# Layernorm sums as three full products, a reordered convolution input, ordered spreads and new keys in a two-layer metaformer on one core

## The chip, the cores and the metric

The kernel runs on one core of one Trainium2 chip, in one launch. The metric is the device time in microseconds, the median of several runs. A core has five engines that run beside each other, each in the order of its own instruction list: TensorE (PE: matrix products, with weight loads shown apart as PEld), VectorE (DVE), ScalarE (ACT), GpSimd (POOL) and SyncE (SP), which here issues every DMA.

## The reference, cut to what matters

The input x is (8, 384, 32, 32) in float32. Everything is float32.

```python
# layer 0
x = x + L0_conv(ln_c(x), ...)           # a selective state space ("mamba") over the 1024 positions
t = to_tokens(x)
t = t + L0_ffn(ln_t(t), W1, b1, W2, b2)  # binarized weights, activations scaled by groups
x = from_tokens(t, x)
# layer 1
x = x + L1_conv(ln_c(x), offset)         # a shift per channel group, then a 5x5 Gauss filter
t = to_tokens(x)
t = t + L1_ffn(ln_t(t), W1, b1, W2, b2)
x = from_tokens(t, x)

def ln_c(v, eps=1e-6):                   # over the 384 channels; ln_t is the same with 1e-5
    m = mean(v, axis=1); s = var(v, axis=1)
    return (v - m) / sqrt(s + eps)

# the recurrence of L0_conv, for 768 inner channels d and 16 states n
dA = exp(dt_t[..., None] * A)
h = dA * h + (dt_t * u_t)[..., None] * B_t[:, None, :]
y = einsum('bdn,bn->bd', h, C_t)
```

The feed-forward part (FFN) works in five groups of the batch; the group size is 8 // 5 = 1, so its scaled output is zero for the last three images, and these need only the two convolutions.

## The kernel before, in words

Nothing is issued where it is written. A class Flow records each operation with its engine, the time that the author books for it, the buffers that it reads and writes, and a key; `Flow.run` then lays all operations out by a list schedule, engine by engine, and issues them in that order. In `run` the waiting operation with the smallest key goes next on its engine, provided its buffers can be had. Among equal keys the loop goes on to the end, so the one recorded last is taken. An operation that needs another table of ScalarE is charged a penalty (PEN) and may be held back for a while (HOLD). On the chip each engine then follows its list and waits on semaphores.

Keys are counted in scans. The state space is cut into 16 units (8 images, two halves of T = 512 positions). A unit has 6 channel blocks (JC) of 128, each with 4 groups of states (NG), so 24 scans a unit and 384 in all. A scan (`scan`) does two pairs p: POOL multiplies `t = dus * bc` (L868), ACT computes four decays (L878), DVE runs four recurrences (L893), POOL (L914) or DVE (L927) multiplies by C, and PE adds up four narrow products into y (L935). There are five t buffers, and a scan takes two.

dt and dt*u of a channel block lie as 128 channels and are needed as 32 channels repeated over four state groups. `spread` (L787) does that through DRAM: one DMA out to `via`, then eight back, four for each of the two pairs p, all with one key; it is called for dts and for dus, for two blocks at a time (`prep`).

Around the scans, all the rest is fitted in by keys: input projections (L645), for the last six units done early (`early`, L723) and kept in DRAM, the output projection (`end`, L997), and for each image the FFNs (first products L1386, second L1465) and the shifted convolution (`conv`). ROWS and CONVS give the key ranges of these per image; UNITS shifts four events of each unit and is all zeros.

`layernorm` (L491) sums over 384 channels on PE. A tile has 128 partitions and three chunks of channels, so `total` (L458) multiplies each chunk by a 128x32 block of ones, into three groups of 32 partitions of one PSUM bank (L464); ACT copies the 96 partitions to SBUF (L477); a second product with `pick`, which has ones in rows 0, 32 and 64, adds the three and spreads the result over all 128 partitions (L484). `layernorm` calls `total` twice, for the mean, which DVE then subtracts (L498), and for the squares that ACT makes (L512); ACT then takes Ln and Exp (L521, L529) and DVE multiplies (L537). There are 52 layernorms.

`conv` turns each 32x32 image by DVE's transposes of 32x32 blocks (L1569), multiplies by a matrix for the shift and filter along one axis (`ups`, L1601: two products of 256 columns), turns it back (L1615), multiplies for the other axis (`overs`, L1629: four of 128 columns), turns it once more (L1642), and POOL adds it to the residual (L1652). The tile `xt` that `ups` reads lies as (y, c) with c = 32, and `ups` reads it as (c, y): neighbours in its order are 32 elements apart. `overs` reads 16 neighbours at a time.

Of the kernel before, what the change touches and what calls it, by code (L numbers as in the profile page):

```python
# [17 lines left out]
P = 128  # L18
# [18 lines left out]

KB, KE, KC_, KY, KG = -0.73, 4.53, 0.68, -3.95, -25.21  # L40

KP, KR = -4.7, 10.49
KEND, KZ, KL, KX, KXP = 1.3, 23.33, -31.97, -2.16, -4.45

KI, KJ = 196.21, 703.54
EZ, EZ0, EZ1 = 6, -56.93, 53.6

AP, AD, AA, AL = 41.75, -45.76, -50.69, -258.62

PEN = 8.61  # L50

GBS = 260.0


ROWS = [
    [15.34, -7.72, -143.06, 131.51, -3.17, 59.74, -84.96, -78.05],
    [94.3, 121.48, 131.64, -65.6, 211.87, 125.27, 265.88, 164.43],
    [164.72, 212.1, 341.92, 181.75, 145.72, 247.03, 303.52, 178.27],
    [227.6, 313.23, 335.93, 52.96, 178.3, 308.14, 239.43, 298.28],
    [299.47, 295.45, 361.88, 314.75, 306.17, 351.8, 603.44, 450.53],  # L60
]
CONVS = [
    [202.4, 111.11],
    [759.94, 953.69],
    [430.57, 41.38],
]


UNITS = [
    [0.0, 0.0, 0.0, 0.0],  # L70
    [0.0, 0.0, 0.0, 0.0],
    [0.0, 0.0, 0.0, 0.0],
    [0.0, 0.0, 0.0, 0.0],
    [0.0, 0.0, 0.0, 0.0],
    [0.0, 0.0, 0.0, 0.0],
    [0.0, 0.0, 0.0, 0.0],
    [0.0, 0.0, 0.0, 0.0],
    [0.0, 0.0, 0.0, 0.0],
    [0.0, 0.0, 0.0, 0.0],
    [0.0, 0.0, 0.0, 0.0],  # L80
    [0.0, 0.0, 0.0, 0.0],
    [0.0, 0.0, 0.0, 0.0],
    [0.0, 0.0, 0.0, 0.0],
    [0.0, 0.0, 0.0, 0.0],
    [0.0, 0.0, 0.0, 0.0],
]


# [65 lines left out]
class Flow:  # L154
# [1 line left out]


    SWITCH = 1.5
    HOLD = {"exp": 0.0, "silu": 8.77, "gelu": 2.31, "softplus": 0.0}

    def __init__(self, nc):
        self.nc, self.ops, self.key, self.filler = nc, [], 0.0, None
# [200 lines left out]
def metaformer_flow(ctx, tc, x, mw, f0, offset, f1, out):  # L363
# [24 lines left out]
    op("POOL", 2.0, lambda e: make_identity(nc, ident.ap), (), [ident])  # L388


    pick = one("pick", [P, P])

    def first_rows(e):
        e.memset(pick.ap, 0.0)
        for q in range(Q):
            e.memset(pick.ap[q * D : q * D + 1, :], 1.0)

    op("POOL", 1.0, first_rows, (), [pick])


    mm = ring("mm", [P, T], 3, ps, ordered=False)
    y_r = ring("y", [P, T], 1, ps)
# [55 lines left out]
    def total(src, acc, sq):  # L458

        def chunks(eng):
            for k in range(KC):
                eng.matmul(  # L464
                    acc.ap[k * D : (k + 1) * D, :],
                    ones.ap[:, :D],
                    src.ap[:, k, :],
                    start=True,
                    stop=True,
                    tile_position=(0, k * D),  # L470
                )

        op("PE", 1.0, chunks, [ones, src], [acc], hold=[sq])
        op(
            "ACT",
            0.6,
            lambda eng: eng.copy(sq.ap[: KC * D, 0, :], acc.ap[: KC * D, :]),  # L477
            [acc],
            [sq],
        )  # L480
        op(
            "PE",
            1.0,
            lambda eng: eng.matmul(  # L484
                acc.ap, pick.ap[: KC * D, :], sq.ap[: KC * D, 0, :], start=True, stop=True
            ),
            [pick, sq],
            [acc],
        )

    def layernorm(tn, e):  # L491

# [69 lines left out]
    def load_x(i):  # L562
# [4 lines left out]
            return  # L567
        dma(lambda: t.ap, lambda: halves(x[b], s), (), [t], 768)

    fl.key = -60  # L570
    load_x(0)
    dma(lambda: cw.ap, lambda: conv_w.rearrange("(j p) t -> p j t", p=P), (), [cw], 10)

    def small(dst, src):
# [211 lines left out]

    def spread(src, r):  # L787

        via = via_r.new()
        dma(lambda: via.ap, lambda: src.ap, [src], [via])  # L790
        dst = [r.new(Q), r.new(Q)]
        for p in range(2):
            for q in range(Q):
                dma(
                    lambda p=p, q=q: dst[p].ap[q * D : (q + 1) * D],
                    lambda p=p: via.ap.rearrange("(c d) t -> d c t", d=D)[:, 2 * p : 2 * p + 2, :],
                    [via],
                    [dst[p][q]],
                    128,
                )  # L800
        return dst

    def prep(i, a):
# [204 lines left out]
    def state_space():  # L1008
        def at(i, j, g=0.0):
            fl.key = i * UNIT + j * NG + g  # L1010

        fl.key = -50
        ln(0)
        n0 = len(fl.ops)
        for j in range(JC):
            xin(0, j)
        weights.extend([o for o in fl.ops[n0:] if o.eng == "SP"][-1:])
        x_proj(0)
        n0 = len(fl.ops)
        load_bc(0, 0)  # L1020
        fl.key = -48
        prep(0, 0)
        started.extend(o for o in fl.ops[n0:] if o.eng == "SP" and o.key == -48)
        fl.key = -46
        n0 = len(fl.ops)
        for g in range(1, NG):
            load_bc(0, g)
        fl.key = -5
        zin(0, 0)
        zin(0, 1)  # L1030
        loads.extend(o for o in fl.ops[n0:] if o.wait == 0 or o.key == -46)
        for i in range(len(units)):
            nxt = i + 1 if i + 1 < len(units) else None
            for j in range(JC):
                for g in range(NG):
                    scan(i, j, g)
                    at(i, j, g)
                    if g == NG - 1 and j % 2 and i * JC + j + 1 < len(units) * JC:
                        fl.key += KP + UNITS[i][0]
                        prep(*divmod(i * JC + j + 1, JC))  # L1040
                        at(i, j, g)
                    if j == 0 and i > 0 and g == 0:
                        fl.key += KEND + UNITS[i][3]
                        end(i - 1)
                        at(i, j, g)
                    if j == 0 and g in (0, 2):
                        fl.key += KZ
                        zin(i, 2 + g)
                        zin(i, 3 + g)
                        fl.key -= KZ  # L1050
                    if nxt:
                        if j == 1 and g == 0:
                            fl.key += KL + UNITS[i][1]
                            load_x(nxt)
                            if nxt < LATE:
                                ln(nxt)
                            at(i, j, g)
                        if j in (2, 3, 4) and g in (0, 1):
                            fl.key += KX + UNITS[i][2]
                            xin(nxt, 2 * (j - 2) + g)  # L1060
                            at(i, j, g)
                        if j == 4 and g == 2:
                            fl.key += KXP + UNITS[i][2]
                            x_proj(nxt)
                            at(i, j, g)
                        if j == JC - 1:
                            load_bc(nxt, g)
                        if j == JC - 1 and g == 1:
                            fl.key += KZ
                            zin(nxt, 0)  # L1070
                            zin(nxt, 1)
                            fl.key -= KZ
                fl.key = i * UNIT + j * NG + NG + KG
                gate(i, j)
        end(len(units) - 1)


    def binarize(w, dst, kc, o):
# [6 lines left out]
        for g in range(NQ):  # L1085
# [40 lines left out]
                lambda e, z=z, s=s: e.activation(s.ap[:, :flat], z.ap[:, :flat], AF.Sign),  # L1126
                [z],
                [s],
            )
            op(  # L1130
                "POOL",
# [414 lines left out]
    def conv(src, dst, dst_ap):  # L1546

        xt = [hb_r.new(2) for _ in range(KC)]
        for s in range(NS):
# [14 lines left out]
            for c in range(KC):  # L1564
# [2 lines left out]
                    "DVE",  # L1567
                    0.7,
                    lambda e, c=c, tn=tn, ys=ys: e.transpose(  # L1569
                        xt[c].ap.rearrange("p (y c) -> p y c", c=32)[:, ys, :],  # L1570
                        tn.ap[:, c, :].rearrange("p (y x) -> p y x", x=32),
                    ),
                    [tn],
                    [xt[c][s]],
# [1 line left out]
        for c in range(KC):  # L1576
# [18 lines left out]
            for h in range(2):  # L1595
                acc = mm.new()

                def ups(e, lt=lts[0], acc=acc, h=h, c=c):
                    for k in (0, 1):
                        cs = slice(h * 16 + k * 8, h * 16 + k * 8 + 8)  # L1600
                        e.matmul(  # L1601
                            acc.ap.rearrange("p (c y) -> p c y", y=32)[:, k * 8 : k * 8 + 8, :],
                            lt.ap[:, 2 * h + k, :],
                            xt[c].ap.rearrange("p (y c) -> p c y", c=32)[:, cs, :],
                            start=True,
                            stop=True,
                        )

                op("PE", 1.0, ups, [lts[0], xt[c]], [acc], hold=[tr])
                hs = slice(h * T, (h + 1) * T)  # L1610

                op(
                    "DVE",
                    0.7,
                    lambda e, tr=tr, acc=acc, hs=hs: e.transpose(  # L1615
                        tr.ap[:, hs].rearrange("p (c x) -> p c x", x=32),
                        acc.ap.rearrange("p (c y) -> p c y", y=32),
                    ),
                    [acc],
                    [tr[h]],  # L1620
# [1 line left out]
            for h in range(2):  # L1622
# [3 lines left out]
                def overs(e, lt=lts[1], acc=acc, xs=xs, tr=tr):  # L1626
# [7 lines left out]
                            stop=True,  # L1634
                        )

                op("PE", 1.3, overs, [lts[1], tr], [acc])

                op(
                    "DVE",  # L1640
                    0.85,
                    lambda e, c=c, acc=acc, xs=xs: e.transpose(  # L1642
                        xt[c].ap.rearrange("p (x y) -> p x y", y=32)[:, xs, :],
                        acc.ap.rearrange("p (c x) -> p x c", x=16),
# [3 lines left out]
                )  # L1648
            op(
                "POOL",  # L1650
                2.35,
                lambda e, xr=xr, c=c: e.tensor_add(  # L1652
                    xr.ap.rearrange("p (y x) -> p y x", x=32),
                    xr.ap.rearrange("p (y x) -> p y x", x=32),
# [106 lines left out]
```

## Time and profile before

The three runs gave 3698.68, 3707.25 and 3713.39 us, the median being 3707.25.

| | us |
|---|---|
| profiled execution, its own time | 3705.44 |
| its span, first to last instruction | 3703.7 |
| mean granted TensorE clock, as a share of full speed | 0.923 |
| HBM read and written | 578.45 MB and 196.48 MB, 209 GB/s |

One execution was profiled. In its groups of instructions a line is the line of the kernel, or that of a helper that records: all DMAs of `dma` have L217, and most table loads L359. "out<-in" names what is written and read. A group's row ends with the idle time of its engine just before its instructions, and what ended it. PE's records overlap, so a group's busy time, in which overlaps count once, is less than its count times its mean. By stretches of the span, busy us of each engine:

| stretch, us | PE | DVE | ACT | POOL | clock |
|---|---|---|---|---|---|
| 0 to 78.6 (before the first scan) | 40.30 | 18.72 | 38.46 | 20.29 | 0.83 |
| 78.6 to 300 | 164.10 | 177.80 | 155.64 | 179.16 | 0.81 |
| 300 to 1000 | 594.77 | 588.38 | 508.20 | 621.70 | 0.91 |
| 1000 to 2000 | 900.20 | 844.96 | 702.93 | 874.83 | 0.95 |
| 2000 to 3000 | 862.04 | 874.36 | 671.94 | 877.58 | 0.93 |
| 3000 to 3634 | 572.93 | 547.48 | 405.90 | 562.72 | 0.94 |
| 3634 to 3703.7 (after the last scan) | 54.76 | 34.94 | 11.64 | 20.70 | 0.93 |

### The profile page before, as it was taken

Reading aid. Unit: us, or ns where it says so; the run is one execution under the profiler, and the core shown is the slowest. Engines: PE = TensorE matmul, PEld = TensorE weight load, DVE = VectorE, ACT = ScalarE, POOL = GpSimd, SP = SyncE. Lnnn points to the kernel's source line nnn. Section 1 sums busy time; section 2 is a strip of 40 time slices with the busy share of each in tenths; the row PEclk is TensorE's granted clock in tenths of the full one; section 3 lists DMA queues with packets and bytes.
Section 4 is the critical chain, followed back from the end, with each engine's and each line's share of the span. In section 5 each row is a group of like instructions: output and inputs, shape, how many; then the busy total and the mean of one; then the engine's idle time right before and its main releaser. Section 6 shows DMA issues by size and latency. Waiting matters only on the chain.

```text
span 3703.7 us, 35888 instructions
## 1 busy us (share of the span) xinstructions
PE 3189.1 (86%) x9572; PEld 1143.7 (31%) x9572; DVE 3086.6 (83%) x3080; ACT 2494.7 (67%) x3661; POOL 3157.0 (85%) x1680
## 2 busy tenths in 40 slices
PE   4777878987999897899979789998877999878988
PEld 1222223322333231333323233332223333323334
DVE  2798888878778889997987899889898888788986
ACT  4767886757667676677768757767665676765562
POOL 3879999897697998888899887989998788997893
PEclk7888979998999897999989899999988999988999
DMA  5858778696686886668587776969776787976964
GB/s 145 184 154 223 198 199 221 184 256 181 207 245 175 231 224 181 200 199 243 177 248 205 196 221 193 244 198 255 228 216 195 209 246 225 257 217 207 270 185 155
DMA packets 680820, 777.44 MB, mean 210 GB/s; under 512 B 113689, under 2 KB 434089, under 8 KB 680617
## 3 DMA queue, kind: packets, MB, share of 16 engines
q1 hardware_dynamic: 680616, 775.14, 74.4%
q8 instruction: 77, 1.26, 0.1%
q14 instruction: 127, 1.03, 0.1%
HBM read 578.45 MB, written 196.48 MB: 209 GB/s over the span
## 4 chain that ended last, share of the span: by engine, by line
PE 39%; DVE 16%; DMA 15%; POOL 12%; ACT 10%; issue 6%; SPq 2%; POOLq 0%; DVEq 0%; ACTq 0%
PE mm L1386 10%; PE mm L1465 9%; POOL t L868 8%; PE mm L645 6%; DVE dp L893 5%; PE y L935 4%; DMA dus<-via 3%; PE mm L997 3%; DVE t L893 3%; POOL t L914 3%; DVE t L927 3%; DMA dts<-via 2%; ACT L359 2%; ACT dp L878 2%; PE mm L1601 2%
## 5 line engine op out<-in xcount | busy, mean ns | idle before, releaser
L868 POOL TENSOR_TENSOR t<-dus,bc 128x1024 f32<-128x1024 f32 x768 | 1797.8, 2361 | 209.9 <-PE y L935 169.6
L914 POOL TENSOR_TENSOR t<-t,bc 128x1024 f32<-128x1024 f32 x384 | 906.8, 2362 | 99.6 <-DVE t L893 89.6
L935 PE MATMUL y<-t,sel 128*32 128x512 f32 x3072 | 554.9, 652 | 184.4 <-DVE t L927 117.8
L1465 PE MATMUL mm<-hb,w 128*128 128x512 f32 x1440 | 675.4, 609 | 28.4 <-DMA w<-w2d 12.1
L1386 PE MATMUL mm<-tn,w 128*128 128x512 f32 x1440 | 670.9, 611 | 24.7 <-DMA w<-w1d 7.5
L878 ACT ACTIVATE da<-dts,aneg 128x512 f32<-128x512 f32 x768 | 520.6, 684 | 240.7 <-DVE t L893 216.0
L878 ACT ACTIVATE dp<-dts,aneg 128x512 f32<-128x512 f32 x768 | 528.3, 688 | 207.2 <-DVE t L927 190.3
L893 DVE TENSOR_TENSOR_SCAN dp<-dp,h,t 128x512 f32<-128x512 f32 x384 | 491.3, 1279 | 71.7 <-ACT dp L878 53.5
L893 DVE TENSOR_TENSOR_SCAN dp<-dp,t 128x512 f32<-128x512 f32 x384 | 468.4, 1220 | 90.6 <-ACT dp L878 59.8
L893 DVE TENSOR_TENSOR_SCAN t<-da,h,t 128x512 f32<-128x512 f32 x384 | 481.2, 1267 | 64.2 <-POOL t L868 59.6
L893 DVE TENSOR_TENSOR_SCAN t<-da,t 128x512 f32<-128x512 f32 x384 | 458.2, 1206 | 79.5 <-POOL t L868 68.5
L359 ACT ACT_TABLE_LOAD x391 | 501.7, 1283 | 6.5
L645 PE MATMUL mm<-xn,win 128*128 128x512 f32 x900 | 439.3, 631 | 39.6 <-DMA win<-in_L_conv_in_proj_w 20.5
L927 DVE TENSOR_TENSOR t<-dp,bc 128x1024 f32<-128x1024 f32 x384 | 465.4, 1212 | 8.8 <-ACT h L920 4.0
L1465 PEld LDWEIGHTS mm<-hb,w 128*128 128x128 f32 x1440 | 264.9, 192 | 431.8 <-issue 352.7
L1386 PEld LDWEIGHTS mm<-tn,w 128*128 128x128 f32 x1440 | 269.4, 193 | 413.8 <-issue 311.5
L997 PE MATMUL mm<-z,wo 128*128 128x512 f32 x552 | 276.6, 634 | 12.2 <-DMA wo<-in_L_conv_out_proj_w 7.6
L645 PEld LDWEIGHTS mm<-xn,win 128*128 128x128 f32 x900 | 173.6, 200 | 294.7 <-issue 209.7
L1398 ACT ACTIVATE he<-mm,b 128x512 f32<-128x512 f32 x240 | 162.9, 680 | 148.9 <-PE mm L1386 141.6
L935 PEld LDWEIGHTS y<-t,sel 128*32 128x32 f32 x3072 | 83.4, 112 | 560.0 <-DVE t L927 201.1
L920 ACT COPY h<-dp 128x2 f32<-128x2 f32 x192 | 30.5, 159 | 218.4 <-DVE t L927 112.6
L1408 DVE TENSOR_REDUCE sm<-he 128x1 f32<-128x1024 f32 x120 | 144.3, 1203 | 30.8 <-ACT he L1398 30.2
(133 smaller groups left out, 3170.5 us busy)
## 6 DMA issues: line engine op xcount, KB each, us to landing
dts<-via SPq DMA_DIRECT2D x768, 128.0 KB, 4.4
dus<-via SPq DMA_DIRECT2D x768, 128.0 KB, 4.5
hd<-he SPq DMA_DIRECT2D x120, 512.0 KB, 4.7
hb<-hd SPq DMA_DIRECT2D x120, 512.0 KB, 5.9
via<-soft SPq DMA_DIRECT2D x192, 256.0 KB, 4.3
w<-w2d SPq DMA_DIRECT2D x120, 384.0 KB, 4.7
w<-w1d SPq DMA_DIRECT2D x240, 192.0 KB, 3.9
bc<-bcd SPq DMA_DIRECT2D x256, 128.0 KB, 4.7
```

Of the source, the lines that this page charges most:

```text
L359: nc.scalar.preload_act_table_set(SETS[table])
L645: e.matmul(acc.ap, w.ap[:, k, :], xn.ap[:, k, :], start=(k == 0), stop=(k == KC - 1))
L868: lambda e, t=t, du=du: e.tensor_mul(t.ap, du.ap, wide(0)),
L878: lambda e, c=c, r=r, dt=dt: e.activation(decay(c), dt.ap[:, r, :], AF.Exp, scale=aneg.ap[:, j * Q + c, g : g + 1],),
L893: e.tensor_tensor_scan(t.ap[:, r, :] if p == 0 else decay(c), decay(c), t.ap[:, r, :], 0.0 if s == 0 else hst[j][p].ap[:, g, r : r + 1], A ...
L914: op("POOL", 2.35, lambda e, t=t: e.tensor_mul(t.ap, t.ap, wide(1)), [bc], [t])
L927: lambda e, t=t: e.tensor_mul(t.ap, da[2].ap, wide(1)),
L935: e.matmul(y.ap[c * D : (c + 1) * D, :], sel.ap, ts[c // 2].ap[:, c % 2, :], start=(g == 0), stop=(g == NG - 1), tile_position=(0, c * D),)
L997: e.matmul(o.ap, flat()[:, j, :], zs[j].ap, start=(j == 0), stop=(j == JC - 1))
L1386: e.matmul(acc.ap, w.ap[:, k, :], tn.ap[:, k, :], start=(k == 0), stop=(k == KC - 1),)
L1398: lambda e, he=he, r=r, m=m, acc=acc: e.activation(he.ap[:, r, :], acc.ap, AF.Identity, bias=b1.ap[:, m : m + 1]),
L1465: e.matmul(acc.ap, w.ap[:, part * 2 + r, :], hs[m // 2].ap[:, r * T : (r + 1) * T], start=(m == 0), stop=(m == MC - 1),)
```

## The change

- `total` becomes three products of 128x128 ones with the three chunks, added up in one PSUM bank. The copy on ACT, the product with `pick` and `pick` itself go. The operation is booked at 1.83 us, where the two before were booked at 1.0 each.
- In `conv` the first transposes write `xt` as (k, y, c) with k = 4 and c = 8, so that `ups` reads 256 neighbours; the next transposes take `ups`' output in the new order. Some booked times around them change.
- In `spread` the eight DMAs get keys that rise with p, and those of dus come after those of dts of the same p. The first x load gets a key of its own, in front of the small weights.
- Sign in `binarize` is recorded as a user of the "exp" table.
- All the constants that shift keys, ROWS, CONVS, UNITS, PEN and HOLD get new values.

```diff
-KB, KE, KC_, KY, KG = -0.73, 4.53, 0.68, -3.95, -25.21
...
-PEN = 8.61
+KB, KE, KC_, KY, KG = -1.16, 5.28, 0.54, -7.6, -27.33
...
+PEN = 12.5
...
 UNITS = [
-    [0.0, 0.0, 0.0, 0.0],
...
+    [-1.66, -2.67, 2.76, -14.73],
+    [-2.83, 6.5, 1.53, 11.27],
...
-    HOLD = {"exp": 0.0, "silu": 8.77, "gelu": 2.31, "softplus": 0.0}
+    HOLD = {"exp": 0.0, "silu": 8.77, "gelu": 3.56, "softplus": 0.82}
...
-    pick = one("pick", [P, P])
...
     def total(src, acc, sq):
         def chunks(eng):
             for k in range(KC):
-                eng.matmul(
-                    acc.ap[k * D : (k + 1) * D, :],
-                    ones.ap[:, :D],
-                    src.ap[:, k, :],
-                    start=True,
-                    stop=True,
-                    tile_position=(0, k * D),
-                )
-
-        op("PE", 1.0, chunks, [ones, src], [acc], hold=[sq])
-        op(
-            "ACT",
-            0.6,
-            lambda eng: eng.copy(sq.ap[: KC * D, 0, :], acc.ap[: KC * D, :]),
-            [acc],
-            [sq],
-        )
-        op(
-            "PE",
-            1.0,
-            lambda eng: eng.matmul(
-                acc.ap, pick.ap[: KC * D, :], sq.ap[: KC * D, 0, :], start=True, stop=True
-            ),
-            [pick, sq],
-            [acc],
-        )
+                eng.matmul(acc.ap, ones.ap, src.ap[:, k, :], start=(k == 0), stop=(k == KC - 1))
+
+        op("PE", 1.83, chunks, [ones, src], [acc], hold=[sq])
...
+    fl.key = -62
+    load_x(0)
     fl.key = -60
-    load_x(0)
...
     def spread(src, r):
-        via = via_r.new()
+        via, k0 = via_r.new(), fl.key
         dma(lambda: via.ap, lambda: src.ap, [src], [via])
         dst = [r.new(Q), r.new(Q)]
         for p in range(2):
+            fl.key = k0 + 0.02 * p + (0.01 if r is dus_r else 0.0)
             for q in range(Q):
...
+        fl.key = k0
         return dst
...
                 lambda e, z=z, s=s: e.activation(s.ap[:, :flat], z.ap[:, :flat], AF.Sign),
                 [z],
                 [s],
+                table="exp",
...
-                        xt[c].ap.rearrange("p (y c) -> p y c", c=32)[:, ys, :],
-                        tn.ap[:, c, :].rearrange("p (y x) -> p y x", x=32),
+                        xt[c].ap.rearrange("p (k y c) -> p y k c", k=4, c=8)[:, ys],
+                        tn.ap[:, c, :].rearrange("p (y a b) -> p y a b", a=4, b=8),
...
                     for k in (0, 1):
-                        cs = slice(h * 16 + k * 8, h * 16 + k * 8 + 8)
                         e.matmul(
-                            acc.ap.rearrange("p (c y) -> p c y", y=32)[:, k * 8 : k * 8 + 8, :],
+                            acc.ap[:, k * 256 : k * 256 + 256],
                             lt.ap[:, 2 * h + k, :],
-                            xt[c].ap.rearrange("p (y c) -> p c y", c=32)[:, cs, :],
+                            xt[c].ap[:, (2 * h + k) * 256 : (2 * h + k + 1) * 256],
...
-                op("PE", 1.0, ups, [lts[0], xt[c]], [acc], hold=[tr])
+                op("PE", 0.75, ups, [lts[0], xt[c]], [acc], hold=[tr])
...
-                        tr.ap[:, hs].rearrange("p (c x) -> p c x", x=32),
-                        acc.ap.rearrange("p (c y) -> p c y", y=32),
+                        tr.ap[:, hs].rearrange("p (k c x) -> p k c x", k=2, x=32),
+                        acc.ap.rearrange("p (k y c) -> p k c y", k=2, c=8),
```

## The prediction

> **What bounds the kernel now.** First the page: busy shares, then the slices.
>
> ```profile
> PE 3189.1 (86%) x9572; PEld 1143.7 (31%) x9572; DVE 3086.6 (83%) x3080; ACT 2494.7 (67%) x3661; POOL 3157.0 (85%) x1680
> ...
> PE   4777878987999897899979789998877999878988
> ...
> POOL 3879999897697998888899887989998788997893
> PEclk7888979998999897999989899999988999988999
> ...
> PE 39%; DVE 16%; DMA 15%; POOL 12%; ACT 10%; issue 6%; SPq 2%; POOLq 0%; DVEq 0%; ACTq 0%
> ```
>
> Three engines are busy 83 to 86% and none fills the span of 3703.7 us: POOL, whose work the change leaves alone, is idle 547 us. So the time is POOL's 3157 us plus what POOL, PE and DVE lose by waiting for one another. The last line, the chain that ended last, runs over PE most (39%). The slices show where nothing can overlap: POOL's first slice is 3 and its last is 3. TensorE's clock is granted at 0.7 to 0.9 where PE has holes and at 9 where it is dense[...].
>
> Then the list of waits: who waited for whom, us in all, times, longest.
>
> ```profile
> POOL t L868 <- PE y L935: 169.6, 86, 8.4
> ...
> ACT sq L477 <- PE mm L464: 61.6, 36, 9.6
> ...
> PE mm L484 <- ACT sq L477: 37.9, 41, 2.0
> ```
>
> POOL's largest loss, 169.6 us, is for the y products: PE works in order, and what stands in front of a y product keeps t buffers from POOL. The other two lines are the layernorm sum's bounce, PE to ACT to PE. Then the groups, kept apart by shape (busy us, mean ns | idle before):
>
> ```profile
> L1386 PE MATMUL mm<-tn,w 128*128 128x512 f32 x1440 | 670.9, 611 | 24.7 <-DMA w<-w1d 7.5 <-DVE tn L537 6.4 <-ACT he L1398 4.4
> ...
> L359 ACT ACT_TABLE_LOAD x391 | 501.7, 1283 | 6.5
> ...
> L645 PE MATMUL mm<-xn,win 128*128 128x512 f32 x900 | 439.3, 631 | 39.6 <-DMA win<-in_L_conv_in_proj_w 20.5 <-DVE xn L537 4.5 <-DVE tr L1535 3.8
> ...
> L484 PE MATMUL mm<-sq,pick 96*128 96x512 f32 x208 | 128.3, 702 | 39.5 <-ACT sq L477 37.9 <-ACT h L920 1.5
> ...
> L1601 PE MATMUL mm<-hb,lt 128*128 128x256 f32 x192 | 89.2, 615 | 13.0 <-DVE hb L1569 8.4 <-DVE hb L1642 4.1 <-DVE xn L498 0.5
> ...
> L464 PE MATMUL mm<-sq,ones 128*32 128x512 f32 x312 | 64.2, 691 | 34.9 <-ACT sq L512 30.7 <-ACT tail L663 2.8 <-ACT soft L824 0.8
> ...
> L477 ACT COPY sq<-mm 96x512 f32<-96x512 f32 x104 | 60.1, 577 | 64.9 <-PE mm L464 61.6 <-PE y L935 1.5 <-ACT soft L824 0.6
> ...
> L464 PE MATMUL mm<-tn,ones 128*32 128x512 f32 x246 | 53.5, 731 | 31.8 <-DMA tn<-in_x 14.0 <-DMA tn<-x 9.7 <-ACT z L746 4.2
> L1629 PE MATMUL mm<-hb,lt 128*128 128x128 f32 x384 | 52.9, 289 | 7.3 <-DVE hb L1615 3.2 <-ACT dp L878 1.3 <-DVE hb L1642 0.9
> ```
>
> Every product leaves two records, so counts are halved below, and the mean of a record is no price: busy us over products is.
>
> **Part 1, the sums (104 of them, two in each of 52 layernorms).** Removed: three narrow products and one with pick. Their busy time is 64.2 + 53.5 + 14.5 (the third L464 row, on xn) + 128.3 = 260.5 us, 2.50 us a sum. Added: three full products, for which the trace has the same form. L1386: 670.9 us over 240 triples = 2.80 us. L645, with its second row of 16.6 us: 455.9 over 156 = 2.92 us. L723, more often cold: 120.1 over 36 = 3.34 us. I take L645, whose triples stand alone among scans as the sums do: 104 x (2.92 - 2.50) = **+44 us of PE**; the ends are +31 and +87. Here a rule speaks against the change: the Trainium skill (TensorE: Matmul & The Clock Gate, Part 3, row/col tiling) says narrow column tiles run concurrently and gives three of 32 columns at N=512 a speedup of 2.38. In this trace a warm narrow triple lasts 1.06 us; 2.38 x 1.06 = 2.52 us for the full one, and less the 1.06 and 1.02 of what goes that is +46 us. The timeline's warm full triples last 2.74 us, +69 us. All agree that PE gets more work.
>
> What it buys: ACT loses 104 copies, 60.1 us; PE's in-order wait for the copy (37.9 us idle) goes, and so does ACT's own 61.6 us idle for L464. From first narrow record to last pick record the timeline shows 2.9 us at best, 4.7 us in the cold start and over 10 us where pick stands behind other work (983.64 to 995.5); after, one piece of 2.7 to 5.3 us. What is late next is layernorm's DVE pass (L498) and Square, unchanged. On the path I count PE's +44 less the hole of 38, at PE's 39% of the chain: +2 us, and for the sooner sums -10 us (ends -40, 0): **-8 us**.
>
> **Part 2, convolution's first product (48 groups of two).** Before, its moving operand is read one element in 32. L1601 has 256 columns a record and takes 615 ns, as much as the 611 of 512 columns in L1386; L1629, which reads runs of 16, takes 289 for 128. So the stride, I conclude, halves the rate. A group now costs 89.2/48 = 1.86 us; in runs, by L1629's 52.9/384 = 0.14 us per record of 128, 4 x 2 x 0.14 = 1.1 us, by half of L1386's stream about 0.9. I take 0.95: 48 x 0.91 = **-44 us of PE**, ends 0 (the stride is not the cause) and -46. It weighs more than its size, since these groups come in convolution's bursts, where PE, DVE and POOL hand one tile round:
>
> ```profile
> 3683.51 3.47 PE mm L1601 x8
> 3687.77 1.16 PE mm L1629 x8
> 3688.93 3.71 PE mm L1601 x8
> 3694.36 2.78 POOL hb L1652
> ```
>
> These are pieces of the chain at its end; in the chain from 3560 us on L1601 alone holds 11.3%. Ten groups stand after the last y product. On the path I take half of the 44: **-22 us**. The transposes around it change pattern, not count. L1642 already reads PSUM with a step of 16 in 692 ns, L1615 without one in 706; I cost them at nothing (ends -2 and +10 us).
>
> **Part 3, the start.** Of equal keys the later recorded goes first, so the first x is now eighth on SP's queue:
>
> ```profile
> 5.20 0.55 SPq L217 DMA_DIRECT2D xn<-in_x  x1
> ...
> 10.87 1.93 PE L464 MATMUL mm<-xn,ones 128*32 128x512 f32 x6 [10.87 <-DMA xn<-in_x]
> ```
>
> With a key of its own it is issued first, at 0.74 us: -4.5 us on a stretch in which all wait for it. The small loads it passes (cw, cb, aneg) are wanted from 20 us on. Two cold sums cost about 2 x 0.6 us more. **-3 us.**
>
> **Part 4, ordered spreads.** By the same rule the second halves (p = 1) of dts and dus were issued before the first, which the scan needs first. Four issues of a median 0.42 us stand between: up to 1.7 us a tensor. The direct waits are small: DMA dus 8.6 us on POOL, dts 16.5 on ACT. I take -6 us, ends 0 and -25, the sum of those waits. No DMA is added.
>
> **Part 5, keys and table loads.** The program's order has 411 table loads for 396: 15 x 1.283 = +19 us of ACT. The skill (ScalarE: Activation LUTs, What ACT_TABLE_LOAD costs) adds a drain, 2.66 us a switch, which would be +40; but L359 shows 6.5 us idle before all 391, so 19 it is, inside ACT's 33% of idle: +3 us on the path at a load's share. In the order, PE has less behind the last y product: two sums instead of four, and 40 over products instead of 48. That is about 4 x 2.08 - 2 x 2.74 + 8 x 0.14 x 2 = 5 us, most in the tail: -4 us. The rest of the keys moves work between units of scans; instruction totals are equal, so I take 0, with ends of -60 and +60: about a third of the 169.6 us that POOL waits for y, either way.
>
> **Sum:** -8 - 22 - 3 - 6 + 3 - 4 = -40 from the profiled run's own 3705.4 us (its span of 3703.7 plus 1.7 around it), hence about 3665; part of any gain is usually lost to the next wait, so I forecast **3670 us**. The profiled run is 1.8 us under the median of 3707.25.
>
> **Rivals.**
> A, hidden: PE's +44 and -44 cancel, and ACT's relief is worth nothing at 67%. For it: the totals of POOL and DVE stay. Against: L1601 is on the chain, the start is too. Time: only the start and the tail, 3698.
> B, slower: full sums block the y products. The recording layer books a sum at 1.83 us but the same form at 2.65, so each is about 0.9 us longer than the order allows for; 104 x 0.9 = 94 us of PE lateness, of which POOL, waiting for y, pays two thirds: +60 us, against -32 from parts 2 to 5: 3733. It decides once POOL's wait for y exceeds 230 us. Against: the booked bounce was also too short, by ACT's queue.
> C, larger gain: the keys pay -50 more: POOL's wait for y falls under 120 us and PE's clock rises; 3620.
>
> **Numbers.** Forecast 0.45 (own range 3645 to 3688), C 0.15, A 0.18, B 0.22. Measurement of this kernel tells 0.5% (18.5 us about 3707) from no change. The forecast and C are faster, 0.60; A same, with B's better edge, 0.20; the rest slower, 0.20. The range takes C's middle and B's: 3615 to 3735.
>
> **What would show it.** Sums: triples of 2.8 to 3.0 us, no copy, ACT near 2455 us. Convolution: its 256-column record well under 615 ns. Start: the first sum by 7 us. Tail: under 65 us after the last scan's product, where the timeline now has 70 (3633 to 3703.7). Keys: POOL's wait for y near 150 us. I am wrong if the 256-column record stays above 550 ns, or if POOL's wait for y grows.

## The result, and the profile after

The kernel became slower: the median of four runs is 3748.64 us (3741.54 to 3754.14) against 3703.43 us (3698.68 to 3713.39) before, a ratio of 1.0121 [1.0101, 1.0141], or 45 us. (Before has a fourth run now, of 3699.61 us, which moves its median from 3707.25. The brackets behind a ratio are its 95% interval. A ratio is taken from all runs of both kernels, so it is not quite that of the two medians.) The forecast of 3670 us had the sign wrong.

The profiled execution took 3741.54 us, the lowest of the four, with a span of 3739.8. These lines of its page answer to the first lines shown of before: the busy shares, and the slices of PE, POOL and the clock.

```profile
PE 3196.0 (85%) x9364; PEld 1200.6 (32%) x9364; DVE 3088.2 (83%) x3080; ACT 2466.3 (66%) x3572; POOL 3156.2 (84%) x1675
...
PE   5877878988999896899989689997869898878897
...
POOL 3779999877877997979798987899988788988894
PEclk7898999999999898999999799997979999989998
```

PE's total rose by 7 us, and those of POOL and DVE stayed within 2 us. The span rose by 36.1 us. So the engines are busy for about as long as before and wait longer. For PE that is a balance: the sums added 72 us, the convolution's product took 34 away, and the y products' busy time fell by 40, though their records are as many and as long, so that more of them overlap:

```profile
L935 PE MATMUL y<-t,sel 128*32 128x512 f32 x3072 | 554.9, 652 | 184.4 <-DVE t L927 117.8 <-POOL t L914 58.1 <-DVE z L959 6.4
```

```profile
L905 PE MATMUL y<-t,sel 128*32 128x512 f32 x3072 | 515.3, 649 | 181.8 <-DVE t L897 86.3 <-POOL t L884 71.1 <-DVE z L929 20.8
```

(The chain that ended last breaks off in this profile, its shares adding up to a fifth of the span, so nothing is read from it.) The list of waits gives the wait, who waited for whom, us in all, times, longest:

```profile
POOL t L838 <- PE y L905: 204.9, 91, 12.1
...
PE mm L454 <- ACT sq L479: 31.9, 14, 3.4
```

POOL waits 204.9 us for the y products, where it was 169.6: +35 us, about what the span lost. The layernorm bounce is gone: the second line is only the products' wait for the squares. The groups by shape (busy us, mean ns | idle before):

```profile
L359 ACT ACT_TABLE_LOAD x410 | 526.0, 1283 | 6.8
L454 PE MATMUL mm<-sq,ones 128*128 128x512 f32 x312 | 162.9, 663 | 34.5 <-ACT sq L479 31.9 <-DVE xr L970 0.9 <-DVE tr L1506 0.8
L454 PE MATMUL mm<-tn,ones 128*128 128x512 f32 x246 | 135.5, 694 | 42.4 <-DMA tn<-in_x 14.8 <-DMA tn<-x 9.9 <-DVE tr L1506 9.1
...
L1571 PE MATMUL mm<-hb,lt 128*128 128x256 f32 x192 | 55.1, 434 | 20.9 <-DVE hb L1540 13.8 <-DVE dp L863 3.0 <-DVE hb L1612 1.2
...
L1612 DVE STREAM_TRANSPOSE hb<-mm 128x512 f32<-128x512 f32 x48 | 33.1, 695 | 8.9 <-PE mm L1599 8.9
L1585 DVE STREAM_TRANSPOSE hb<-mm 128x512 f32<-128x512 f32 x48 | 32.7, 695 | 7.3 <-PE mm L1571 6.7
...
L454 PE MATMUL mm<-xn,ones 128*128 128x512 f32 x66 | 34.4, 662 | 7.2 <-DMA xn<-in_x 5.4 <-DVE tn L504 0.8 <-ACT da L848 0.7
```

The sums cost 162.9 + 135.5 + 34.4 = 332.8 us, 3.20 us each. The convolution's first product fell from 615 to 434 ns a record, from 89.2 to 55.1 us.

Where did the time go? POOL's first product of the scans (L868, now L838) marks the stages. Its answers, before and then after, give durations in ns (min/median/max) and the first and last start:

```profile
L868 POOL TENSOR_TENSOR t<-dus,bc x768: 2330/2357/3070, 78.6 to 3621.8; 128x1024 f32<-128x1024 f32 x192
```

```profile
L838 POOL TENSOR_TENSOR t<-dus,bc x768: 2329/2356/3087, 73.3 to 3670.9; 128x1024 f32<-128x1024 f32 x192
```

The scans start 5.3 us sooner. What follows the last of these products shrank from 3703.7 - 3621.8 = 81.9 to 68.9 us. The stretch between grew from 3543.2 to 3597.6 us, **+54.4**. Start and tail gained 18 us, and the stretch in which all else is fitted in among the scans lost three times that.

### The profile page after: what moved, and what is told of

It reads as the page before. It is cut to its first block, busy times and chain, and to the rows that moved or that the text cites. A ratio compares the mean times of both kernels' runs of the same rounds, so it can differ in the third digit from the quotient of the medians.

```text
span 3739.8 us, 35315 instructions
## 1 busy us (share of the span) xinstructions
PE 3196.0 (85%) x9364; PEld 1200.6 (32%) x9364; DVE 3088.2 (83%) x3080; ACT 2466.3 (66%) x3572; POOL 3156.2 (84%) x1675
## 5 line engine op out<-in xcount | busy, mean ns | idle before, releaser
L838 POOL TENSOR_TENSOR t<-dus,bc 128x1024 f32<-128x1024 f32 x768 | 1796.6, 2359 | 262.8 <-PE y L905 204.9
L1436 PE MATMUL mm<-hb,w 128*128 128x512 f32 x1440 | 688.4, 617 | 53.6 <-ACT hb L1412 19.3
L905 PE MATMUL y<-t,sel 128*32 128x512 f32 x3072 | 515.3, 649 | 181.8 <-DVE t L897 86.3
L905 PEld LDWEIGHTS y<-t,sel 128*32 128x32 f32 x3072 | 74.0, 111 | 534.6 <-issue 184.0
L454 PE MATMUL mm<-sq,ones 128*128 128x512 f32 x312 | 162.9, 663 | 34.5 <-ACT sq L479 31.9
```

The source lines that it names most:

```text
L454: eng.matmul(acc.ap, ones.ap, src.ap[:, k, :], start=(k == 0), stop=(k == KC - 1))
L838: lambda e, t=t, du=du: e.tensor_mul(t.ap, du.ap, wide(0)),
L905: e.matmul(y.ap[c * D : (c + 1) * D, :], sel.ap, ts[c // 2].ap[:, c % 2, :], start=(g == 0), stop=(g == NG - 1), tile_position=(0, c * D),)
L1436: e.matmul(acc.ap, w.ap[:, part * 2 + r, :], hs[m // 2].ap[:, r * T : (r + 1) * T], start=(m == 0), stop=(m == MC - 1),)
```

## The experiments

The changed kernel differs in two ways: in what its operations issue, and in the order in which the schedule lays them. That order hangs on every key and every booked time. So the experiments come in two kinds. In the ones called **order kept**, all keys, penalties and booked times of before stay, the schedule is laid as before, and only what an operation issues differs (an operation that is no longer needed issues nothing). In the others the schedule is laid anew. Three theories stood before the first four runs: the prediction's rival B, the longer sums; the new keys; and a third, called FIT, which took over after them: constants fit one order of one kernel, any order laid anew costs a per cent or more, and the new constants fit the new kernel, but not as well as the old ones fitted the old kernel.

**The sums alone, order kept.**

```diff
-                eng.matmul(acc.ap[k * D : (k + 1) * D, :], ones.ap[:, :D],
...
+                eng.matmul(acc.ap, ones.ap, src.ap[:, k, :], start=(k == 0), stop=(k == KC - 1))
...
-            lambda eng: eng.copy(sq.ap[: KC * D, 0, :], acc.ap[: KC * D, :]),
+            lambda eng: None,
...
-            lambda eng: eng.matmul(acc.ap, pick.ap[: KC * D, :], ...
+            lambda eng: None,
```

> The kernel before with its order kept to the letter: the layernorm sum's first PE operation issues three full products, the copy and the product with pick issue nothing, and no booked time or key changes. Theory SUMS (full products in front of the y products make POOL wait): 25 to 60 us slower than before, POOL's wait for y from 170 to over 200 us. Theory KEYS (the sums are harmless, the new keys lay out a worse order): within 15 us of before, or faster by up to 30. Theory FIT (before's constants fit its own order, and any order laid anew is about 1% worse): as KEYS, since the order is kept.

3723.99 us against 3707.08, ratio 1.0056 [1.0034, 1.0078], +21 us (17 between the medians). POOL's wait for y in its list of waits:

```profile
POOL t L859 <- PE y L926: 190.3, 102, 9.2
```

From 169.6 to 190.3 us, with PE's total up from 3189.1 to 3235.4 (the profiled execution was the longest of its five, 3737.66 us). Rival B's mechanism is there, at a third of the 60 us that it was given. The sums' busy time rose by 70 us (161.6 + 131.8 + 37.1 against 260.5) and PE's total by 46 only: the granted clock was 0.931 to 0.933 in these five runs and 0.919 to 0.926 in those of before, and a record of the y products took 640 ns instead of 652.

**The convolution's input alone, order kept** (the diff is that of the change: `xt` as (k, y, c), the product on 256 neighbours, the next transpose to match).

> The kernel before with its order kept, and only convolution's first input in runs of eight (and the transposes on both sides of it in the matching pattern). All theories: 192 records of 256 columns fall from 615 to about 434 ns, 34 us of PE. My prediction's share on the path was half of the gain: 15 to 25 us faster. If PE is not what ends the waits here: 0 to 8 us faster.

3694.95 us, ratio 0.9974 [0.9962, 0.9987], -10 us (-12 between the medians). Its group:

```profile
L1600 PE MATMUL mm<-hb,lt 128*128 128x256 f32 x192 | 55.7, 432 | 15.8 <-DVE hb L1569 8.3 <-DVE hb L1641 5.6 <-DVE xn L537 0.8
```

The group lost 34 us of PE, and the end came 10 us sooner.

**Before's operations with all the new constants, and the changed operations with all the old ones** (ROWS, CONVS, UNITS and PEN too). Both lay a new order.

```diff
-KB, KE, KC_, KY, KG = -0.73, 4.53, 0.68, -3.95, -25.21
+KB, KE, KC_, KY, KG = -1.16, 5.28, 0.54, -7.6, -27.33
...
-    HOLD = {"exp": 0.0, "silu": 8.77, "gelu": 2.31, "softplus": 0.0}
+    HOLD = {"exp": 0.0, "silu": 8.77, "gelu": 3.56, "softplus": 0.82}
```

> The kernel before with all the constants of the change (keys, ROWS, CONVS, UNITS, PEN, HOLD) and nothing else. SUMS: within 20 us of before, either way. KEYS: 40 us slower or more. FIT: 20 to 60 us slower, because these constants belong to other durations.

> The changed kernel with all the constants of before. SUMS: as slow as the changed kernel, 30 to 60 us slower than before. KEYS: no slower than before, and up to 35 us faster (the gains of my parts 1 to 4). FIT: 20 to 60 us slower than before, as the old constants don't fit the new booked times.

3823.27 us (1.0322 [1.0302, 1.0342]) and 3793.47 us (1.0243 [1.0221, 1.0264]). Each mixture is slower than both kernels. So the new keys are not bad in themselves: with the new operations they give 1.0121, better than the old keys do. But neither run tells a bad key from one that doesn't fit, which the next four do.

**One constant of before, nudged.** KE is the key of a scan's decays on ACT, in scans; AP is added to the keys of PE's part of the FFN and convolution work; the third edit puts right a booked time, that of the convolution's addition on POOL, which takes 2.88 us.

```diff
-KB, KE, KC_, KY, KG = -0.73, 4.53, 0.68, -3.95, -25.21
+KB, KE, KC_, KY, KG = -0.73, 4.73, 0.68, -3.95, -25.21
...
-AP, AD, AA, AL = 41.75, -45.76, -50.69, -258.62
+AP, AD, AA, AL = 42.75, -45.76, -50.69, -258.62
...
-                2.35,
+                2.85,
```

> The kernel before with one constant moved: KE, the key of the decays on ACT, from 4.53 to 4.73, a fifth of a scan. Nothing that a single instruction does changes, only the order. FIT (the constants fit one order; any order laid anew is worse): 15 to 100 us slower. NO FIT (orders near each other are equally good, only the large step of all constants to the wrong kernel hurts): within 10 us of before.

> The kernel before with one constant moved: AP, which shifts the FFN's and convolution's work on PE, from 41.75 to 42.75 scans. FIT: 15 to 100 us slower. NO FIT: within 10 us of before.

> The kernel before with one booked time put right: convolution's sum on POOL booked at 2.85 us, as the change does it and as the trace shows it (2.88), where 2.35 stood. FIT: 10 to 80 us slower although the booking is truer. NO FIT, or truer bookings give better orders: within 10 us, or up to 20 us faster.

3832.66 us (1.0347 [1.0319, 1.0376]), 3776.81 (1.0191 [1.0169, 1.0214]) and 3784.52 (1.0208 [1.0181, 1.0234]). A nudge that means nothing costs 1.9 to 3.5%, and a truer booked time costs 2% as well. Each was moved in one direction only, so whether the other direction loses too isn't shown. The page of the first, and two of its waits, with the second of them before:

```profile
PE 3225.8 (84%) x9572; PEld 1152.5 (30%) x9572; DVE 3088.7 (81%) x3080; ACT 2500.4 (65%) x3662; POOL 3159.4 (83%) x1680
```

```profile
POOL t L868 <- PE y L935: 217.7, 87, 22.0
...
DVE dp L893 <- ACT dp L878: 167.9, 105, 8.5
```

```profile
DVE dp L893 <- ACT dp L878: 113.4, 90, 5.3
```

The picture is that of the changed kernel, larger: the same instructions on PE, DVE and POOL as before, their totals equal but for 37 us of PE, POOL waiting 48 us longer for y and DVE 55 us longer for its decays. The 37 us of PE go with a lower granted clock, 0.913 against 0.923: 1.1% of 3189 us is 35. But POOL's wait for y is not where every order loses. In the changed kernel with the old constants, at 1.0243, and with truer bookings (next), at 1.0165, it was no longer than the 169.6 us of before:

```profile
POOL t L838 <- PE y L905: 165.0, 102, 8.9
```

```profile
POOL t L838 <- PE y L905: 168.0, 85, 27.5
```

In the first of these, POOL waited for DVE instead: 128.4 us for the states of its second product, where it was 89.6, and 119.6 us for those that it copies on, where it was 74.6.

**The changed kernel with truer booked times**: a sum at 2.65 us instead of 1.83, `ups` at 1.0 us instead of 0.75.

> The changed kernel with the sum booked at 2.65 us for 1.83 (what the same form is booked at elsewhere) and the first convolution product at 1.0 for 0.75. If the false booking is what costs (the order lets y products run into the long sums): 20 to 45 us faster than the changed kernel, that is 3700 to 3730. FIT: slower than the changed kernel, 3760 or more, since its constants were fitted to the false booking.

3766.0 us, 1.0165 [1.0138, 1.0191]: no better than the change itself, and rather slower, though the two intervals just overlap. Booking the sums right doesn't mend it, since that lays another order, which nothing has been fitted to.

**Both operations together, order kept.**

> The kernel before with its order kept, full sums and convolution's input in runs together. If the parts simply add in a fixed order (sums +0.56%, runs -0.26%): 1.003 of before, 3710 to 3725 us, so that the rest of the changed kernel's loss lies in the order. If the full sums and the shorter convolution products share their waits: outside 3700 to 3735.

3707.88 us against 3705.66, 1.0007 [0.999, 1.0023]. Sums and convolution cancel. The change as made differs from this run by its constants and bookings, its start and its spreads, and it is 1.0121/1.0007 = 1.0114, some 42 us, slower. POOL's wait for y shows the same:

```profile
POOL t L859 <- PE y L926: 173.7, 93, 8.9
```

Of the 35 us by which it grew with the change, the two operations account for 4, and the rest came with the new order.

**Start and spreads, order kept**: the first x load goes first on SP, and the eight places that a spread's DMAs have in SP's list go to p = 0 and then p = 1.

```diff
+        at = {o.n: i for i, o in enumerate(out)}
+        for mine in self.sets:
+            for i, o in zip(sorted(at[o.n] for o in mine), mine):
+                out[i] = o
+        out.sort(key=lambda o: o.n != self.first)
```

> The kernel before with its order kept, but for SP's own list: the first x load is issued first, and within each spread the eight places go to the first pair's four loads and then to the second pair's. My prediction: 3 us for the x load and 6 for the spreads, 5 to 12 us faster. If the waits for these loads are ended by something else: the x load alone, 0 to 5 us faster.

3706.28 us, 1.0011 [0.9995, 1.0028]: nothing. The timeline of PE shows that the start itself came as planned:

```profile
6.00 1.93 PE L470 MATMUL mm<-xn,ones 128*32 128x512 f32 x6 [6.00 <-DMA xn<-in_x]
```

The first sum starts at 6.00 us instead of 10.87, and the first scan product at 77.0 instead of 78.6. The rest of the 4.9 us was lost within the first stage; the remaining 1.6 are less than these runs can tell. (The change also puts the dus loads of a pair behind its dts loads. This run leaves that as it was, so it counts as order below.)

**The parts that don't cost, order kept**: the convolution's input, the first x load and the spreads, with before's narrow sums.

> The kernel before with its order kept, convolution's input in runs of eight, the first x load first and ordered spreads; narrow sums and all constants stay. FIT, with the parts adding in a fixed order: 10 to 25 us faster than before, 3680 to 3697, and faster than the changed kernel by 50 or more.

3691.89 us, 0.9964 [0.9949, 0.998]. It is faster than both kernels, by 14 us against before. Most of that is the convolution's 10.

**The changed kernel, nudged**: AP from 38.47 to 39.47.

> The changed kernel with one constant moved, AP from 38.47 to 39.47, as was done with the kernel before. If the changed kernel's constants are fitted to it as those of before are to the other: 30 to 130 us slower than the changed kernel, 3780 to 3880. If its constants are an unfitted set among many: within 30 us of the changed kernel, to either side.

3821.18 us, 1.0312 [1.0278, 1.0345], 2% slower than the changed kernel itself. So the new constants do fit the new kernel, as far as one nudge can tell.

**Shorter sums in both orders.** Here each sum leaves out the product with the third chunk of channels. The schedule doesn't see it, so each kernel keeps its own order; a sum then takes 2.26 us (115.4 + 94.8 + 25.1 over 104), nearer the 1.83 that the changed kernel books.

```diff
-            for k in range(KC):
-                eng.matmul(acc.ap, ones.ap, src.ap[:, k, :], start=(k == 0), stop=(k == KC - 1))
+            for k in range(KC - 1):
+                eng.matmul(acc.ap, ones.ap, src.ap[:, k, :], start=(k == 0), stop=(k == KC - 2))
```

> The changed kernel, order and constants kept, with each layernorm sum made of two of its three products (the third chunk is left out, so a sum takes about as long as the 1.83 us that it is booked at). If the sums' overrun past their booking is what costs in the changed order: 30 to 55 us faster than the changed kernel, 3695 to 3720. If the order itself is the worse one: 5 to 25 us faster, as in the control.

> The control: the kernel before with its order kept, convolution's input in runs, and sums of two products instead of three (the third chunk left out), which fit into the room of what they replace. Both theories: 5 to 25 us faster than the same with three products (3707.9), 3683 to 3703.

3720.06 us in the new order (1.0039 [1.0021, 1.0057]) and 3684.84 in the old (0.9954 [0.9934, 0.9974]), against 3703.05. The new order gained 1.0121 - 1.0039 = 0.82% and the old 1.0007 - 0.9954 = 0.53%. The difference, 0.3% or some 10 us, is what overlong sums cost the new order more than the old; with the four intervals it isn't told from none. What remains between the orders is 1.0039 - 0.9954 = 0.85%, some 31 us, with sums of the same length (2.30 us in the old order). Start and spreads, the other difference, were worth nothing above. So that part is the order's. POOL's wait for y was 191.2 us in the new order and 172.6 in the old.

The granted clock goes with the order too. For each set of operations, every order laid anew had a lower one than the order of before: 0.907 to 0.916 against 0.917 to 0.927 for before's operations, 0.917 to 0.927 against 0.930 to 0.934 for the changed ones, and 0.916 to 0.922 against 0.923 to 0.929 with the shorter sums. Whether that is a cause of the loss or comes of PE's longer idle time isn't shown.

How an order loses time is seen in the fifth unit of scans, from its first POOL product to that of the next unit: 1006 to 1239 us before, 1018 to 1275 after, 233 and 257 us. It is the one that lost most; nine of the sixteen units became longer, by up to 24 us, and seven shorter, by up to 14. With the shorter sums it took 253 us in the new order and 235 in the old, so the sums' length is not what it lost. POOL's wait for y in it, before and then after:

```profile
POOL t L868 <- PE y L935: 15.6, 6, 8.3
```

```profile
POOL t L838 <- PE y L905: 27.4, 7, 12.1
```

PE's groups in it, before:

```profile
L1465 PE MATMUL mm<-hb,w 128*128 128x512 f32 x144 | 66.2, 600 | 2.3 <-ACT hb L1441 1.1 <-DMA w<-w2d 1.1
L1386 PE MATMUL mm<-tn,w 128*128 128x512 f32 x138 | 63.7, 601 | 5.7 <-DVE tn L537 4.4 <-ACT z L746 1.3
```

and after:

```profile
L1436 PE MATMUL mm<-hb,w 128*128 128x512 f32 x164 | 78.2, 623 | 5.1 <-DMA w<-w2d 2.8 <-ACT hb L1412 1.5 <-ACT he L1369 0.6
L1357 PE MATMUL mm<-tn,w 128*128 128x512 f32 x144 | 68.3, 621 | 1.7 <-DVE sm L1308 0.9 <-ACT he L1369 0.8
...
L454 PE MATMUL mm<-sq,ones 128*128 128x512 f32 x12 | 5.6, 601 | 0.0
L454 PE MATMUL mm<-tn,ones 128*128 128x512 f32 x6 | 2.8, 610 | 0.0
L454 PE MATMUL mm<-xn,ones 128*128 128x512 f32 x6 | 2.7, 592 | 0.0
```

The sums take 11.1 us of this stretch (four of them; before, five took 10.6). The FFN's products take 146.5 us where they took 129.9. The new keys laid 26 records more of them (308 against 282) beside the same 24 scans, in a stretch in which PE was busy 216.8 of 233 us already. At the 0.46 us that a record cost before, that is 12 of the 16.6 us; the rest are longer records, at a clock of 0.95 against 0.99. The longest of POOL's waits for y falls here. PE's timeline up to it (start, us, what; the last line is POOL's):

```profile
1135.19 2.74 PE L1357 MATMUL mm<-tn,w 128*128 128x512 f32 x6
...
1138.17 2.84 PE L613 MATMUL mm<-xn,win 128*128 128x512 f32 x6
1140.85 2.74 PE L1357 MATMUL mm<-tn,w 128*128 128x512 f32 x6
1145.02 2.81 PE L613 MATMUL mm<-xn,win 128*128 128x512 f32 x6 [1.43 <-DMA win<-in_L_conv_in_proj_w]
1147.76 1.06 PE L905 MATMUL y<-t,sel 128*32 128x512 f32 x8
```

```profile
1148.91 9.30 POOL L838 TENSOR_TENSOR t<-dus,bc 128x1024 f32<-128x1024 f32 x4 [12.15 <-PE y L905]
```

The last t tile of the y product was ready when DVE ended at 1137.6. But PE's list has two input projections and an FFN product in front of it, the second projection waits for its own weights, and POOL gets its buffers back only at 1148.91. No layernorm sum stands there. That is one wait in one unit; how the other units lose or gain isn't shown.

## Why the prediction was wrong, point by point

- **The step that failed** is in part 5: "The rest of the keys moves work between units of scans; instruction totals are equal, so I take 0, with ends of -60 and +60". The totals are equal indeed, but they say nothing of the order, and the order is worth about +42 us, table loads, start and tail included, of which some 10 may be sums that outlast what it booked for them. Zero was the wrong middle for it: eight kernels ran in full in an order laid anew, the change among them, and every one is 1.2 to 3.5% slower than before. The end of +60 covered the change. Which key is to blame isn't shown.
- **The other half of the miss** is in parts 1 to 4. The sum was -40 and the kernel moved by +45, 85 us apart. Part 5 took -1, with table loads and tail, for +42: 43 of them. Parts 1 to 4 took -39 together, and in the old order they came to +3 or so (1.0007 for the operations, nothing told from none for start and spreads). With the order at zero the kernel would have been as fast as before, and not faster.
- **Part 1** took the sums at 2.92 us and -8 us on the path. They took 3.20 us, nearer the 3.34 of the often cold L723, so PE gained 332.8 - 260.5 = 72 us of work instead of 44 (inside the ends of 31 and 87), and alone in the old order they cost +21 us. What the prediction set against PE's time, the hole at the bounce and the sooner sums, didn't pay for it. The trade of the copy and its waits for PE's time is a loss, since the engine it loads is the one that POOL waits for. The prediction's estimate from the Trainium skill on narrow column tiles (TensorE: Matmul & The Clock Gate, Part 3, row/col tiling) was +46; the mean over warm and cold sums is well above its 2.52 us for the triple. ACT was relieved of 28 us (2466.3, where 2455 was forecast), and since the sums lost in the old order even so, the relief didn't pay for them.
- **Part 2** had the mechanism right: the step of 32 elements slowed the product, and the record fell to 434 ns. It didn't halve the rate: a group took 55.1/48 = 1.15 us instead of the 0.95 taken, against 1.86 before, near the 1.1 that the prediction's other estimate gave. So the gain was 34 us of PE and not 44; on the path it was -10, not -22. The transposes at no cost: right, 695 ns both.
- **Part 3 and part 4**: the start came as planned in the trace, and at the end both were worth nothing that can be told: 1.0011 [0.9995, 1.0028], against -3 and -6.
- **Table loads**: 411 instead of 396, as forecast, 15 loads or 19 us of ACT. L359 alone shows 410 instead of 391, since four of the five loads that stood at other lines went to it. Again there is hardly any idle time before them (6.8 us). What they cost at the end is part of the order's 42 us and isn't shown alone. **The tail** was under 65 us: from the end of the last y product, 54 us instead of 68.
- **The signs**: the record fell under 550 ns, but POOL's wait for y grew, by 35 us, which the prediction had named as a sign of being wrong.
- **Rival A** had PE's two sums cancel, and in the old order they do (1.0007); but it too left the order out.
- **Rival B** was 15 us off the time, 3733 against 3748, but not for its own reason. Its mechanism is real (+21 us alone), yet POOL's wait for y stayed at 204.9 us, under the 230 from which it was to decide, and its +60 was three times too large. The convolution pays its real price back (1.0007 for both); what B lacks is the order.

## What to carry to other kernels

Where a planner lays in-order instruction lists from fitted constants, try an edit first in the kept order, which gives the edit's own price, and only then fit anew; a mixture of old constants and new operations tells nothing of either. Nudge one constant that means nothing, to learn what a new order costs by itself (here 1.9 to 3.5%), and don't take zero for a change of keys, penalties or booked times: in this kernel all eight new orders lost. Don't pay for the relief of an idle engine with time on the one whose products free the others' buffers.

## What the runs showed of the hardware

- The same 256-column float32 product took 615 ns a record when its moving operand lay 32 elements apart, and 434 ns in runs of neighbours. In the run of this part alone, where only the layout of what it reads and writes differed, it took 432.
- DVE's transposes from PSUM took the same time with either pattern (695 ns against 706 and 692).
- Full products of a sum took 3.20 us in the mean of 104, though those late in the kernel take some 2.8 us (2.84 and 2.81 for the last two); the first two of the kernel took 4.65 and 5.49 us.
- With full sums for narrow ones, in the same order, the granted clock rose from 0.919 to 0.926 in the runs of before to 0.931 to 0.933. Why isn't shown.
